# A four-layer graph network on one core: the output stages of the fourth layer spread over two chunks

## The chip, the cores and the metric

The kernel runs on one NeuronCore of a Trainium2 chip. A core has five engines that run their own instruction queues and wait for each other by semaphores: TensorE (PE, matrix products into the accumulator memory PSUM), VectorE (DVE), ScalarE (ACT), GpSimd (POOL), and SyncE (SP), which here only issues transfers. DMA queues move data between the device memory and the on-chip buffers. The metric is the device time of one execution in microseconds (us). The time before is the median of three runs.

## The reference

A graph has N = 12,500 nodes with 32 features and E = 400,000 edges from `src` to `dst`, sorted by `dst`. Four message-passing layers follow each other; each one normalizes the node features, computes something for every edge from its source node, sums it over the edges of each target node, and adds the result to the features. The change concerns the fourth, an equivariant convolution with 8 scalars and 8 three-vectors per node:

```python
h = relu(edge_scalars @ (fc_w1 * (1.0 / sqrt(8)))) * SQRT2      # E x 256
w = (h @ (fc_w2 * (1.0 / sqrt(256)))).reshape(E, 4, 8, 8)       # four 8x8 matrices per edge
x = node_features[edge_src]
s1, v1 = x[:, :8], x[:, 8:].reshape(E, 8, 3)
s2, v2 = edge_sh[:, 0], edge_sh[:, 1:4]
out_s = A_S * (einsum('eu,euw->ew', s1 * s2, w[:, 0]) + C * einsum('eui,ei,euw->ew', v1, v2, w[:, 1]))
out_v = A_V * C * (einsum('eu,euw,ei->ewi', s1, w[:, 2], v2) + einsum('eui,euw->ewi', v1 * s2, w[:, 3]))
node_out = segment_sum(concat([out_s, out_v]), edge_dst) * const
```

So each edge has its own 256 weights, made by a small network from 8 numbers, and uses them on the 32 features of its source node.

## The kernel before

The four layers run one after the other. The fourth is `edges3`. It cuts the edges into NW = 196 chunks of 2048: CT = 16 columns of 128 edges, one edge per partition. A Python loop writes out the work of all chunks; a planner (the framework under the kernel) then sets the order of instructions on each engine. It keeps to the order in which they are written where two are ready by its own estimate of the times, and takes a later one first where the earlier isn't ready. A buffer of a pool is taken again when its last reader is done.

The steps of one chunk `c`:

- `fetch` issues four loads on SP's queue: the source indices `src`, the local target places `local` with the first node of the chunk's window behind them (`places_of`, L466), the four numbers per edge `edge_attr`, and the input of the hidden layer `emb`. They go into a pool of 6 buffers (`load3`).
- `gather` issues 16 indirect DMAs on POOL (L1226), one per column: each partition fetches the 32 features of its edge's source node from device memory into `hs`. There are 4 buffers of `hs`.
- `hidden`, in four steps: two matmuls into `ps_h` (L1237; one buffer of PSUM) and a ReLU by ACT into `hid` (L1239).
- `scalars`: four DVE instructions (L1245 `q`, L1247 `dd`, L1249 `q`, L1251 `vv`) multiply the gathered features with `edge_attr`.
- `product`, in four slots of four columns: eight fp32 matmuls (L1262, sixteen records in the trace) make the 256 weights of 512 edges in `ps_w` (two buffers of PSUM); DVE multiplies them with the features: `pa` (L1266), `ps` (L1268), `pv` (L1270). `pa`, `ps` and `pv` of a chunk fill up over the four slots. `ps` is also the last reader of `hs`: the fourth slot's sets the buffer free for the gather of four chunks later.
- `outputs`: DVE reductions of `pa` (L1278), `pv` (L1279) and `ps` (L1282, into `rs`), a product (L1284, `t1`) and a sum (L1286) make `f`, the 32 numbers per edge.
- `thirds`, four steps: `f` is written as three bf16 parts in `f3`. Step 0: ACT rounds `f` to bf16 (L441). Step 1: DVE takes that away from `f` (L443). Step 2: ACT rounds the rest (L441 again). Step 3: DVE takes that away and writes the third part (L445).
- `places`, in four steps of four columns: ACT makes one-hot rows `oh` of the local target place (L1292 four times, L1293 once).
- `collect`, the range sum: 16 matmuls (L1298) of `f3` and `oh` add the chunk's edges into the 128 nodes of its window, in `ps_sum` (one buffer); ACT copies it (L1301).
- `add`, the fold: a matmul (L1304) adds the three parts, ACT copies the result (L1306), and `put_late` (L456) loads the first node of the window into a register of ACT and writes the window to device memory from ACT's queue (L459).

All pools but those named have two buffers (`rs`, `t1` and `dd` one, `wsum` four).

Iteration `c` of the loop (L1318 on) first calls `fetch` for chunk c + 4 and `gather` for c + 2. Then come four slots, s = 0 to 3. In each, chunk c has its `product` and a quarter of its `places`, chunk c - 1 (`last`) has a part of its output stages, and chunk c + 1 has a step of `hidden` (in slot 3 also `scalars`). The output stages of `last` are written so: slot 0 all of `outputs` and step 0 of the thirds, slot 1 the steps 1 and 2, slot 2 step 3 and `collect`, slot 3 `add`. So a chunk's last write comes one iteration behind its products.

The order in which the trace shows them on DVE, in one chunk period: L1278 and L1279 of `last`, the three products of slot 0, L1282, `pa` of slot 1, L1284, `ps` of slot 1, L1286, `pv` of slot 1, L443, the three of slot 2, L445, L1245 and L1247, `pa` and `ps` and `pv` of slot 3, L1249 and L1251. On PE: the range sum of `last`, the last step of `hidden`, the fold, then product, hidden, product, hidden, product, hidden, product.

Of the kernel before, what the change touches and what calls it, by code (L numbers as in the profile page):

```python
# [8 lines left out]
F32 = mybir.dt.float32  # L9
# [3 lines left out]
ALU = mybir.AluOpType  # L13
AX = mybir.AxisListType
PSUM = bass.MemoryType.PSUM

P = 128
D = 32
# [19 lines left out]
class GNN:  # L38
# [424 lines left out]
            c["first"] = self.nc.values_load(c["wbase"], engines=[mybir.EngineType.SP], min_val=0, max_val=self.N - 1)  # L463
        return c["first"]

    def places_of(self, pool, row):  # L466

        t = pool.tile([P, self.CT + 1], F32, name="local")
        self.nc.sync.dma_start(t, self.local[:, ds(row, 1), :].rearrange("p o t -> p (o t)"))
        return {"local": t[:, : self.CT], "wbase": t[0:1, self.CT :].bitcast(I32)}  # L470

# [732 lines left out]
    def edges3(self):  # L1204

        nc, tc, CT = self.nc, self.tc, self.CT
        with ExitStack() as ctx:
            ld = ctx.enter_context(tc.tile_pool(name="load3", bufs=6))
            gp = ctx.enter_context(tc.tile_pool(name="gather3", bufs=4))
            wp = ctx.enter_context(tc.tile_pool(name="work3", bufs=2))  # L1210
# [4 lines left out]
            def fetch(c):  # L1215
                row = c["no"]
                c["src"] = self.load(ld, "src", c["col"])
                c.update(self.places_of(ld, row))
                c["sh"] = self.load(ld, "edge_attr_4", c["col"])
                c["emb"] = ld.tile([72, Q4 * B], BF16, name="emb")  # L1220
                nc.sync.dma_start(c["emb"], self.emb8[:, :, ds(row, 1), :].rearrange("k f o e -> (k f) (o e)"))

            def gather(c):
                c["hs"] = gp.tile([P, CT, D], F32, name="hs")
                for k in range(CT):
                    nc.gpsimd.indirect_dma_start(  # L1226
                        out=c["hs"][:, k, :], out_offset=None, in_=self.feats[3][:],
                        in_offset=bass.IndirectOffsetOnAxis(ap=c["src"][:, k : k + 1], axis=0))
# [13 lines left out]
            def scalars(c):  # L1242
                hs, sh = c["hs"], c["sh"]
                q = c["q"] = wp.tile([P, CT, 16], F32, name="q")
                nc.vector.tensor_mul(q[:, :, 0:8], hs[:, :, 0:8], sh[:, :, 0:1].to_broadcast([P, CT, 8]))  # L1245
                dd = wp.tile([P, CT, 3, 8], F32, name="dd", bufs=1)
                nc.vector.tensor_mul(dd, hs[:, :, 8:32].rearrange("p g (k u) -> p g k u", k=3),  # L1247
                                     sh[:, :, 1:4, None].to_broadcast([P, CT, 3, 8]))
                nc.vector.tensor_reduce(q[:, :, 8:16], dd.rearrange("p g k u -> p g u k"), AX.X, ALU.add)  # L1249
                vv = c["vv"] = wp.tile([P, CT, 3, 8], F32, name="vv")  # L1250
                nc.vector.tensor_mul(vv.rearrange("p g i u -> p g (i u)"), hs[:, :, 8:32], sh[:, :, 0:1].to_broadcast([P, CT, 24]))  # L1251
# [19 lines left out]
                                     w[:, :, None, 192:256].to_broadcast([P, 4, 3, 64]),  # L1271
                                     c["vv"][:, gs].rearrange("p g i u -> p (g i) u")[:, :, None, :].to_broadcast([P, 12, 8, 8]))

            def outputs(c):
                sh = c["sh"]
                f = c["f"] = wp.tile([P, CT, D], F32, name="f")
                fv = f[:, :, 8:32]
                nc.vector.tensor_reduce(f[:, :, 0:8], c["pa"], AX.X, ALU.add)  # L1278
                nc.vector.tensor_reduce(fv.rearrange("p g (w i) -> p g i w", i=3),  # L1279
                                        c["pv"].rearrange("p g i (w u) -> p (g i) w u", u=8), AX.X, ALU.add)  # L1280
                rs = wp.tile([P, CT, 8], F32, name="rs", bufs=1)
                nc.vector.tensor_reduce(rs, c["ps"], AX.X, ALU.add)  # L1282
                t1 = wp.tile([P, CT, 8, 3], F32, name="t1", bufs=1)
                nc.vector.tensor_mul(t1, rs[:, :, :, None].to_broadcast([P, CT, 8, 3]),  # L1284
                                     sh[:, :, None, 1:4].to_broadcast([P, CT, 8, 3]))
                nc.vector.tensor_add(fv, fv, t1.rearrange("p g w i -> p g (w i)"))  # L1286

            def places(c, k0, k1):
                if k0 == 0:
                    c["oh"] = wp.tile([P, CT, P], BF16, name="oh")  # L1290
                for k in range(k0, k1):
                    nc.scalar.activation(c["oh"][:, k, :], self.iota, AF.Square, bias=c["local"][:, k : k + 1], scale=-1.0)  # L1292
                nc.scalar.activation(c["oh"][:, k0:k1, :], c["oh"][:, k0:k1, :], AF.Relu, bias=self.one, scale=-2.0)  # L1293

            def collect(c):
                c["sum"] = ps.tile([P, B], F32, name="ps_sum")
                for k in range(CT):
                    nc.tensor.matmul(c["sum"][: 3 * D, 0:P], lhsT=c["f3"][:, k].rearrange("p i f -> p (i f)"), rhs=c["oh"][:, k, :],  # L1298
                                     start=k == 0, stop=k == CT - 1)
                c["s4"] = wp.tile([3 * D, P], F32, name="s4")  # L1300
                nc.scalar.copy(c["s4"], c["sum"][: 3 * D, 0:P])  # L1301

            def add(c):
                nc.tensor.matmul(c["sum"][:, P : P + D], lhsT=c["s4"], rhs=self.fold[: 3 * D], start=True, stop=True)  # L1304
                s = wp.tile([P, D], F32, name="wsum", bufs=4)
                nc.scalar.copy(s, c["sum"][:, P : P + D])  # L1306
                self.put_late(3, c, s)

            NW = self.NW
            cs = [{"no": c, "col": c * CT} for c in range(NW)]  # L1310
            for c in range(4):
                fetch(cs[c])
# [2 lines left out]
            for s in range(4):  # L1315
                hidden(cs[0], s % 2, s // 2)
            scalars(cs[0])
            for c in range(NW + 1):  # L1318
                now = cs[c] if c < NW else None
                if c + 4 < NW:  # L1320
                    fetch(cs[c + 4])
                if c + 2 < NW:
                    gather(cs[c + 2])
                for s in range(4):
                    if now:
                        product(now, s)
                        places(now, 4 * s, 4 * s + 4)
                    if c:
                        last = cs[c - 1]
                        if s == 0:  # L1330
                            outputs(last)
                            self.thirds(wp, last, 0)
                        elif s == 1:
                            self.thirds(wp, last, 1)
                            self.thirds(wp, last, 2)
                        elif s == 2:
                            self.thirds(wp, last, 3)
                            collect(last)
                        else:
                            add(last)  # L1340
                    if c + 1 < NW:
                        hidden(cs[c + 1], s % 2, s // 2)
                        if s == 3:
                            scalars(cs[c + 1])
# [151 lines left out]
```

## Time and profile before

| what | value |
|---|---|
| median of 3 runs | 20,968.87 us (20,962.72 to 21,010.88) |
| the profiled execution | 20,866.96 us |
| its span in the profile | 20,865.2 us |
| mean granted clock of TensorE | 0.841 |
| PE, DVE, ACT, POOL busy over the whole span | 61%, 61%, 31%, 71% |
| PE, DVE, ACT, POOL busy in the fourth layer (500 us from 17,500 us) | 74%, 65%, 46%, 57% |
| memory traffic in the fourth layer | 23 GB/s |
| matmuls of the products, L1262, per record | 413 ns mean |
| reductions L1278, L1279, L1282 | 2276, 3340, 1206 ns |
| `pa`, `ps`, `pv` (L1266, L1268, L1270) | 686, 413, 946 ns |
| parts of `f`: L441 (ACT), L443, L445 (DVE) | 606, 690, 680 ns |
| one indirect gather, L1226 | 969 ns |

The shares over the whole span mix four layers with different limits, so they say little on this one. The fourth layer begins some 15,500 us after the start. Durations are those of one instruction from its start to its end; on DVE the next one often starts a little before the end is recorded (0.60 us from the start of `pa` to that of `ps`, 0.33 from `ps` to `pv`), and sums along an engine go by these distances. The ends of matmuls are modelled in the records. "remote" as a releaser stands for a wait whose end the profile can't put down to an instruction of this core.

### The profile page before, as it was taken

How to read it: one execution, taken by the hardware profiler on the slowest of the kernel's cores; microseconds unless marked ns; L12 is line 12 of the kernel's file. 1: busy time of each engine (PE TensorE's matmuls, PEld its weight loads, DVE VectorE, ACT ScalarE, POOL GpSimd, SP SyncE). 2: the span in 40 equal slices, each digit the busy share in tenths (PEclk: the TensorE clock that was granted, in tenths of full speed). 3: DMA queues.
4: the chain of work that ended last, by engine and by line, in shares of the span. 5: the costliest groups of instructions: out<-in, count | busy, mean ns of one | idle time of the engine just before them, and what ended most of it. 6: DMA issues, size and time to landing. Idle time of an engine off the chain costs nothing. (4 is left out here: it accounts for less than half of the span.)

```text
span 20865.2 us, 192054 instructions
## 1 busy us (share of the span) xinstructions
PE 12672.2 (61%) x56452; PEld 6857.3 (33%) x56452; DVE 12731.2 (61%) x25514; ACT 6397.8 (31%) x13844; POOL 14767.1 (71%) x12552
## 2 busy tenths in 40 slices
PE   2433433333766666666666666666637777777776
PEld 2333333331211111111111111111125555655554
DVE  3544444334766666666666666666746666666666
ACT  0001110001333333333333333333314444444443
POOL 5777777774788888888888888888855555555554
PEclk9999999998777777777777777777768888888888
DMA  3123332112444444444444444444421111111111
GB/s 96 43 46 109 114 94 74 24 23 67 97 91 91 91 91 91 90 92 89 92 89 89 91 88 91 89 91 90 87 49 23 24 24 24 24 24 24 24 24 30
DMA packets 1541412, 1407.87 MB, mean 67 GB/s; under 512 B 1114278, under 2 KB 1309952, under 8 KB 1485464
## 3 DMA queue, kind: packets, MB, share of 16 engines
q1 hardware_dynamic: 724998, 1146.69, 17.5%
q0 software_dynamic: 752640, 206.32, 12.7%
q10 hardware_dynamic: 62704, 42.42, 0.7%
q8 instruction: 448, 7.34, 0.1%
q14 instruction: 622, 5.10, 0.1%
HBM read 1157.36 MB, written 236.38 MB: 67 GB/s over the span
## 5 line engine op out<-in xcount | busy, mean ns | idle before, releaser
L965 POOL DMA_INDIRECT acc<-summed,rows x3136 | 5167.0, 1648 | 998.0 <-issue 880.2
L1226 POOL DMA_INDIRECT hs<-feat,src x3136 | 3039.5, 969 | 2356.2 <-DVE ps L1268 1354.8
L494 POOL DMA_INDIRECT hs<-feat,src x3136 | 3359.7, 1071 | 1387.8 <-issue 878.5
L766 POOL DMA_INDIRECT hs<-feat,src x3136 | 3200.1, 1020 | 1196.9 <-issue 940.2
L1262 PE MATMUL ps_w<-w2b,hid 128*128 128x256 f32 x12544 | 3191.5, 411 | 63.4 <-issue 50.2
L810 DVE TENSOR_TENSOR z<-ps_y,hid 128x1024 f32<-128x1024 f32 x2352 | 2834.7, 1212 | 382.5 <-PE ps_y L807 153.0
L807 PE MATMUL ps_y<-X,w2t 64*128 64x512 f32 x4704 | 2384.7, 746 | 1113.9 <-DVE z L810 699.9
L1262 PEld LDWEIGHTS ps_w<-w2b,hid 128*128 128x128 f32 x12544 | 2593.3, 209 | 561.4 <-issue 80.6
L807 PE MATMUL ps_y<-Q,w2t 64*128 64x512 f32 x4704 | 1681.0, 842 | 1644.5 <-DVE z L810 994.3
L429 PE MATMUL ps_win<-m,oh 128*128 128x32 f32 x6272 | 1472.5, 400 | 856.8 <-issue 270.8
L441 ACT CAST f<-f 128x512 bf16<-128x512 f32 x784 | 479.8, 612 | 4770.9 <-DVE f L835 3993.4
L817 PE MATMUL ps_o<-z,sums 128*32 128x512 f32 x9408 | 1758.8, 706 | 23.7 <-DVE r L822 15.8
L429 PEld LDWEIGHTS ps_win<-m,oh 128*128 128x128 f32 x6272 | 1396.3, 328 | 928.7 <-issue 576.6
L648 PE MATMUL ps_deg<-olo,ohi 128*125 128x100 bf16 x3136 | 462.4, 298 | 2007.0 <-DVE olo L645 1232.4
L1266 DVE TENSOR_TENSOR pa<-ps_w,q 128x512 f32<-128x512 f32 x784 | 537.6, 686 | 1624.7 <-remote 1274.2
L781 DVE STREAM_TRANSPOSE X<-hs 128x512 f32<-128x512 f32 x392 | 273.4, 700 | 2035.2 <-DMA hs<-feat,src 1719.1
L1239 ACT ACTIVATE hid<-ps_h 128x1024 f32<-128x1024 f32 x784 | 801.8, 1023 | 2259.3 <-remote 1465.7
L807 PEld LDWEIGHTS ps_y<-Q,w2t 64*128 64x128 f32 x4704 | 523.4, 256 | 2889.5 <-issue 1436.1
L807 PEld LDWEIGHTS ps_y<-X,w2t 64*128 64x128 f32 x4704 | 614.8, 210 | 2326.8 <-DVE z L810 1215.7
L621 DVE TENSOR_TENSOR m<-hs,edge_attr 128x128 f32<-128x128 f32 x784 | 225.9, 288 | 1608.5 <-issue 679.8
L622 ACT ACTIVATE m<-m 128x128 f32<-128x128 f32 x784 | 238.9, 308 | 3084.4 <-DVE m L621 1040.1
L648 PEld LDWEIGHTS <-ohi 128*125 128x125 bf16 x3136 | 446.5, 215 | 1995.9 <-DVE ohi L645 931.6
(206 smaller groups left out, 19755.0 us busy)
## 6 DMA issues: line engine op xcount, KB each, us to landing
has<-loc_t SPq DMA_DIRECT2D x392, 1024.0 KB
srow<-in_src_t SPq DMA_DIRECT2D x392, 512.0 KB
hs<-feat,src POOLq DMA_INDIRECT x9408
N<-n_t SPq DMA_DIRECT2D x3136, 32.0 KB
emb<-pp SPq DMA_DIRECT2D x252, 280.0 KB
emb<-emb SPq DMA_DIRECT2D x196, 360.0 KB
emb<-pp SPq DMA_DIRECT2D x252, 224.0 KB
emb<-emb SPq DMA_DIRECT2D x196, 288.0 KB
```

The source lines that it names most:

```text
L429: nc.tensor.matmul(c["sum"], lhsT=oh[:, k, :], rhs=feat[:, k, :], start=t0 + k == 0, stop=t0 + k == self.CT - 1)
L494: self.nc.gpsimd.indirect_dma_start(out=t[:, k, :], out_offset=None, in_=self.feats[l][:], in_offset=bass.IndirectOffsetOnAxis(ap=idx[:, t ...
L648: nc.tensor.matmul(c["deg"][:NP, :J], lhsT=ohi[:, k, :], rhs=olo[:, k, :], start=t0 + k == 0, stop=t0 + k == self.CT - 1)
L766: nc.gpsimd.indirect_dma_start(out=c["hs"][:, k, :], out_offset=None, in_=self.feats[1][:], in_offset=bass.IndirectOffsetOnAxis(ap=c["src" ...
L807: nc.tensor.matmul(y[:, q, :], lhsT=self.w2t[64 * q : 64 * q + 64, h, j, :], rhs=c["Q" if j < 3 else "X"][64 * q : 64 * q + 64, h, :], sta ...
L810: nc.vector.tensor_mul(z, y, c["hid"][:, 2 * h : 2 * h + 2, :])
L817: nc.tensor.matmul(c["o", j // 3][32 * q : 32 * q + 32, :], lhsT=self.sums[:, j, :], rhs=c["z", j, q % 2][:, q // 2, :], start=j % 3 == 0, ...
L965: nc.gpsimd.indirect_dma_start(out=self.tabs[2][k % NTAB][:], out_offset=bass.IndirectOffsetOnAxis(ap=c["rows"][:, G * g + k : G * g + k + ...
L1226: nc.gpsimd.indirect_dma_start(out=c["hs"][:, k, :], out_offset=None, in_=self.feats[3][:], in_offset=bass.IndirectOffsetOnAxis(ap=c["src" ...
L1239: nc.scalar.activation(c["hid"][:, m, :, 2 * h : 2 * h + 2, :].rearrange("p b q s -> p q b s"), t.rearrange("p q (b s) -> p q b s", s=32), ...
L1262: nc.tensor.matmul(w[:, k, :], lhsT=c["hid"][:, m, 4 * g + k].rearrange("p q s -> p (q s)"), rhs=self.w2b[:, m, :], start=m == 0, stop=m == 1)
L1266: nc.vector.tensor_mul(c["pa"][:, gs], w[:, :, 0:128].rearrange("p g (w u) -> p g w u", u=16), c["q"][:, gs, None, :].to_broadcast([P, 4, ...
```

## The change

The output stages of a chunk are written over two iterations in place of one. In iteration c, `now` is chunk c, `last` is c - 1, `prev` is c - 2:

| slot | before: of `last` | after: of `prev` | after: of `last` |
|---|---|---|---|
| 0 | `outputs` (five instructions), thirds 0 | thirds 3 | places 0 to 3, L1278 |
| 1 | thirds 1, thirds 2 | `collect` | places 4 to 7, L1279 |
| 2 | thirds 3, `collect` | `add` | places 8 to 11, L1282, L1284, L1286, thirds 0 |
| 3 | `add` | | places 12 to 15, thirds 1, thirds 2 |

(In the diff L1278, L1279 and so on keep their instructions; the lines get other numbers.) `places` moves from `now` to `last`, a chunk later. In the text of a slot, `prev` comes behind `product` and ahead of `last`. The loop has one more round. `local` gets eight buffers in place of six, since the first node of a window is now read up to an iteration later; all other buffers keep their numbers.

```diff
--- before.py
+++ after.py
@@ -463,9 +463,9 @@
             c["first"] = self.nc.values_load(c["wbase"], engines=[mybir.EngineType.SP], min_val=0, max_val=self.N - 1)
         return c["first"]
 
-    def places_of(self, pool, row):
-
-        t = pool.tile([P, self.CT + 1], F32, name="local")
+    def places_of(self, pool, row, bufs=None):
+
+        t = pool.tile([P, self.CT + 1], F32, name="local", bufs=bufs)
         self.nc.sync.dma_start(t, self.local[:, ds(row, 1), :].rearrange("p o t -> p (o t)"))
         return {"local": t[:, : self.CT], "wbase": t[0:1, self.CT :].bitcast(I32)}
 
@@ -1215,7 +1215,7 @@
             def fetch(c):
                 row = c["no"]
                 c["src"] = self.load(ld, "src", c["col"])
-                c.update(self.places_of(ld, row))
+                c.update(self.places_of(ld, row, bufs=8))
                 c["sh"] = self.load(ld, "edge_attr_4", c["col"])
                 c["emb"] = ld.tile([72, Q4 * B], BF16, name="emb")
                 nc.sync.dma_start(c["emb"], self.emb8[:, :, ds(row, 1), :].rearrange("k f o e -> (k f) (o e)"))
@@ -1271,13 +1271,17 @@
                                      w[:, :, None, 192:256].to_broadcast([P, 4, 3, 64]),
                                      c["vv"][:, gs].rearrange("p g i u -> p (g i) u")[:, :, None, :].to_broadcast([P, 12, 8, 8]))
 
-            def outputs(c):
-                sh = c["sh"]
-                f = c["f"] = wp.tile([P, CT, D], F32, name="f")
-                fv = f[:, :, 8:32]
-                nc.vector.tensor_reduce(f[:, :, 0:8], c["pa"], AX.X, ALU.add)
-                nc.vector.tensor_reduce(fv.rearrange("p g (w i) -> p g i w", i=3),
-                                        c["pv"].rearrange("p g i (w u) -> p (g i) w u", u=8), AX.X, ALU.add)
+            def outputs(c, step):
+
+                if step == 0:
+                    c["f"] = wp.tile([P, CT, D], F32, name="f")
+                    nc.vector.tensor_reduce(c["f"][:, :, 0:8], c["pa"], AX.X, ALU.add)
+                    return
+                sh, fv = c["sh"], c["f"][:, :, 8:32]
+                if step == 1:
+                    nc.vector.tensor_reduce(fv.rearrange("p g (w i) -> p g i w", i=3),
+                                            c["pv"].rearrange("p g i (w u) -> p (g i) w u", u=8), AX.X, ALU.add)
+                    return
                 rs = wp.tile([P, CT, 8], F32, name="rs", bufs=1)
                 nc.vector.tensor_reduce(rs, c["ps"], AX.X, ALU.add)
                 t1 = wp.tile([P, CT, 8, 3], F32, name="t1", bufs=1)
@@ -1315,8 +1319,8 @@
             for s in range(4):
                 hidden(cs[0], s % 2, s // 2)
             scalars(cs[0])
-            for c in range(NW + 1):
-                now = cs[c] if c < NW else None
+            for c in range(NW + 2):
+                now, last, prev = (cs[c - k] if 0 <= c - k < NW else None for k in range(3))
                 if c + 4 < NW:
                     fetch(cs[c + 4])
                 if c + 2 < NW:
@@ -1324,20 +1328,21 @@
                 for s in range(4):
                     if now:
                         product(now, s)
-                        places(now, 4 * s, 4 * s + 4)
-                    if c:
-                        last = cs[c - 1]
+                    if prev:
                         if s == 0:
-                            outputs(last)
-                            self.thirds(wp, last, 0)
+                            self.thirds(wp, prev, 3)
                         elif s == 1:
-                            self.thirds(wp, last, 1)
+                            collect(prev)
+                        elif s == 2:
+                            add(prev)
+                    if last:
+                        places(last, 4 * s, 4 * s + 4)
+                        if s < 3:
+                            outputs(last, s)
+                        if s > 1:
+                            self.thirds(wp, last, s - 2)
+                        if s == 3:
                             self.thirds(wp, last, 2)
-                        elif s == 2:
-                            self.thirds(wp, last, 3)
-                            collect(last)
-                        else:
-                            add(last)
                     if c + 1 < NW:
                         hidden(cs[c + 1], s % 2, s // 2)
                         if s == 3:
```

## The prediction

> **What bounds the kernel now.** First the page's slices (the span in 40 equal parts of 522 us, each digit a busy share in tenths), to find the fourth layer: the last ten digits, from about 15,500 us to the end of its gathers at 20,707 us.
>
> ```profile
> PE   2433433333766666666666666666637777777776
> ...
> DVE  3544444334766666666666666666746666666666
> POOL 5777777774788888888888888888855555555554
> ```
>
> No engine is full there. Four windows of 500 us inside the layer give one picture; a row holds the busy time of PE, PEld, DVE, ACT and POOL:
>
> ```profile
> 17500.00:18000.00 500.00, 370.52 (x1645) 296.21 (x1644) 323.80 (x421) 232.44 (x509) 285.98 (x295) 0.85 0.13 23
> ```
>
> PE is busy 74%, DVE 65%, POOL 57%, ACT 46%. So a ring of waits sets the pace, and I looked for its period and its members. From one chunk's first gather (L1226) to the next is 27.1 us, to a tenth, in chunk after chunk; 196 chunks of it are 5.3 ms. The waits of 2800 us (17,500 to 20,300, 103 chunks; us in total, times, longest):
>
> ```profile
> ACT hid L1239 <- remote: 776.2, 144, 10.3
> POOL hs L1226 <- DVE ps L1268: 723.3, 103, 7.8
> DVE pa L1266 <- remote: 694.8, 149, 9.5
> ...
> PE ps_sum L1298 <- DVE f L445: 545.6, 99, 8.8
> ```
>
> The change aims at the fourth line: PE stands 545.6/103 = 5.3 us per chunk in front of the range sum, because L445 writes the last bf16 part late. What the reader should see is that the other three are longer, and what they are. The timeline of one chunk shows it (start, duration, engine, line; in brackets the wait and its releaser):
>
> ```profile
> 18979.06 0.94 POOL L1226 DMA_INDIRECT hs<-feat,src  x1 [6.77 <-DVE ps L1268]
> ...
> 18989.81 3.62 PE L1262 MATMUL ps_w<-w2b,hid 128*128 128x256 f32 x16
> ...
> 19001.82 0.69 DVE L1266 TENSOR_TENSOR pa<-ps_w,q 128x512 f32<-128x512 f32 x1 [3.85 <-remote]
> 19001.87 1.02 ACT L1239 ACTIVATE hid<-ps_h 128x1024 f32<-128x1024 f32 x1 [4.61 <-remote]
> ...
> 19003.63 0.68 DVE L445 TENSOR_TENSOR f<-f,f 128x512 bf16<-128x512 f32 x1
> ...
> 19004.36 1.94 PE L1298 MATMUL ps_sum<-oh,f 128*96 128x128 bf16 x16 [4.56 <-DVE f L445]
> ...
> 19004.90 0.68 DVE L1266 TENSOR_TENSOR pa<-ps_w,q 128x512 f32<-128x512 f32 x1
> ...
> 19006.18 0.94 POOL L1226 DMA_INDIRECT hs<-feat,src  x1 [7.09 <-DVE ps L1268]
> ```
>
> The third product's matmuls (18989.81) end by the record at 18993.43; DVE takes the result at 19001.82, 8.4 us later, and the profile finds no releaser ("remote"). ACT's hid is let go in the same moment, though its matmuls are long done. In all chunks that I laid over one another, PE results ready later than about 12 us after a chunk's first gather are seen only 22.7 us after it, a moment behind the last of the sixteen gathers (18998.14, 19.08 us after the first, 0.94 long); results ready before 7.6 us are seen at once. From 19001.82 DVE runs pa, ps, pv, L445, two of the scalars (L1245, L1247), pa, ps, and the fourth ps frees the hs buffer for the next first gather: 19006.18 - 19001.82 = 4.4 us. **The ring is 22.7 us (gathers and the late release) + 4.4 us (DVE) = 27.1 us.** A sign that gathers do it: behind the last one (20,707 us) the reductions of L1278 begin at 20714.94, 20734.31 and 20752.11, so chunks of 19.4 and 17.8 us.
>
> The Trainium skill, "Perfetto Trace Analysis", section "Tensor Engine Instruction (MATMUL, LD_WEIGHTS)", says that the profiler estimates a matmul's end and doesn't observe it. By it PE itself could be the slow part, the 5.3 us would come off the period, and the time would be some 1040 us shorter (an estimate), about 19,930. The rows speak against it: the third product's records end at 18993.43 and those of ACT's hid at 18996.34, and both are let go within 0.05 us.
>
> **The change part by part.** Per chunk no instruction, transfer or matmul is added or dropped; all are moved.
>
> (a) PE's wait for L445 goes, 5.3 us per chunk of PE time. PE is not on the ring at that point: it waits while DVE does its 4.4 us. What goes on next is the fourth hidden matmul and the first product of the next chunk, some 3 us earlier; they then wait for PSUM (two ps_w buffers, freed by the third and fourth pv). Gain on the ring as such: 0; what it could give is in the first rival.
>
> (b) L445 goes from the third slot to the first slot of the next iteration. It lies on the 4.4 us with 0.60 us (19003.63 to the next start, 19004.23). Gain 0.60.
>
> (c) DVE's order. Today the planner puts L1278 and L1279 (2.28 + 3.34 us) ahead of the first pa, L1282 behind the first pv, L1284 and L1286 in between the second trio; all five are written in slot 0. The diff writes L1279 one slot and L1282, L1284, L1286 two slots later. Fully as written, L1282 (1.13 to the next start), L1284 and L1286 (0.47 each) stand between the third pv and the fourth pa: +2.07, with (b) +1.5, ring 28.6. If the planner hoists them all as it hoists today's, none of them does: +0, with (b) -0.6, and without L1245 and L1247 (0.20 + 0.47) there too, -1.3, ring 25.8. Between these: it hoists what is ready when its own clock has DVE idle, and it hoisted today by about one slot; so L1282 and L1284 come ahead of the third product and L1286 stays. +0.47.
>
> (d) L443, 0.60 us, follows the first cast (L441), which follows L1286. With L1286 behind the third product, L443 lands before or behind the fourth pa. Before: +0.60. Today it waits 112.0/104 = 1.1 us per chunk for ACT; on the path that wait would count, 0 to 1.1. I take 0.60 and, as an estimate, 0.13 of the wait.
>
> (e) The cast stands in ACT's third slot, 0.61 us (L441), ahead of a hidden's relu (1.02). ACT is busy 46% and itself waits for the release; cost 0 while that covers it. Queued behind a cast that waits for its f are the relu and with it the next ps_h (one buffer) and product. The same section of the Trainium skill calls ACT and DVE strict FIFO, which speaks against the change; in the trace ACT's order is that of its queue, and the sum by the rule is rival 4.
>
> (f) Sum (1.94 us by its records) and fold (0.47) move to the second and third slot, with copies (0.26, 0.18), the register load and the write on ACT's queue (0.34 us issue). Their data are then an iteration old, so nobody waits for them; they push the third product back by up to 2.4 us, which (a)'s earlier start covers. The places (16 + 4 ACT instructions) are a chunk later and lose nothing. The loads on SP keep their order; only "local" has eight buffers.
>
> (g) One more round at the end: its L445, sum, fold and write were serial there already. 0 to 5 us, taken as 0.
>
> Sum: -0.60 + 0.47 + 0.60 + 0.13 = +0.60 us a chunk, x 196 = +118 us. Against the profiled execution, 20866.96 us (span 20865.2, 1.8 around it), that is 20,985. The median of the runs shown is 20,968.87, 0.49% above the profiled one; so 21,087 there, rounded to 21,085. The likeliest case runs from +0.3 (no measurable change ends there) to (c) as written, +1.5 us per chunk: 21,030 to 21,260.
>
> **The rivals.**
>
> 1. *The third product slips through (faster).* PE starts earlier by (a); the third product is ready at 14.4 us in the chunk shown, about 12 would be wanted. Then DVE does the third trio before 22.7 and only the fourth pa and ps (0.60 + 0.41, and 0.27 until POOL starts) follow: 22.7 + 1.3 = 24.0, or -3.1 x 196 = -600 us at most, 20,370; if it does so in four chunks of ten, -240, 20,730. For: ready 2.4 us too late, start 3 us earlier. Against: the sum and fold now lie in front of it, and its PSUM waits for the first pv, which stands behind the 5.6 us of L1278 and L1279.
>
> 2. *All hoisted (faster).* (c)'s lower bound: -1.3 x 196 = -255 us, 20,715. For: today's order. Against: the text now places them lower.
>
> 3. *The same ring.* What enters the 4.4 us equals what leaves it (L443 for L445): within 0.3 us a chunk, within 60 us of 20,969. 0.3% of 20,969 is 63 us, about what a measurement of this kernel can tell from no change.
>
> 4. *Much slower: the first product is caught.* If the planner keeps L1278 and L1279 behind the first two trios and the cast in front of the relu, the hidden and product chain starts later; a first or second product that is ready after 12 instead of before 7.6 is held to 22.7, and the fourth one then runs after the release with a PE at half clock (matmuls 0.43 us apart instead of 0.22, seen after the waits): 16 x 0.21 = 3.4 more for its sixteen records, with the likeliest case's 0.60 +4.0 x 196 = +785 us, 21,755. It decides when the second product is ready beyond 12 us; today 10.5 (18989.54 - 18979.06), seen 3.0 late.
>
> 5. *It doesn't do what it says.* If L445 of prev still runs right before the sum, the wait stays and the ring too: the time of rival 3, counted there.
>
> **How the numbers follow.** Likeliest 0.42, rival 1 0.15, rival 2 0.13, rivals 3 and 5 0.14, rival 4 0.16. Faster by over 0.3%: 0.28; within: 0.14; slower: 0.58. The range leaves out the deepest half of rival 1 and the outer half of rival 4 (if its hold comes in three chunks of four, +590): 20,500 to 21,560.
>
> **What would show it.** Right: the wait of PE for L445 falls from 545.6 to nearly 0 while POOL's for ps stays, first gathers 27.4 to 28.5 us apart, pa and hid still "remote", the third product seen at 22.7, and L443 or L1286 in front of the fourth pa in the timeline. (a) is wrong if the period falls towards 24 with the third pa ahead of the last gather, (c) if all reductions lie before the third pa, (e) and (f) if PE's products start later than now. The prediction is wrong altogether if gathers are not what holds PE's results, for then the freed 5.3 us count.

## The result, and the profile after

| | before | after |
|---|---|---|
| median of 4 runs | 20,979.38 us (20,962.72 to 21,010.88) | 21,485.1 us (21,466.02 to 21,491.9) |
| ratio | | 1.0241, 95% interval 1.0229 to 1.0253 |
| span of the profiled execution | 20,865.2 us | 21,478.9 us |
| from first gather to first gather, fourth layer, mean of 181 chunks | 27.11 us | 30.29 us |
| chunks rounded to 27 or 28 us | 180 | 58 |
| rounded to 29 or 30 us | 1 | 20 |
| rounded to 31 us or more | 0 | 103 |

The change costs 506 us (2.4%), where 116 were forecast. 3.18 us more per chunk x 196 = 623 us, about the 613.7 by which the spans differ. So all of it lies in the fourth layer, and it is not spread evenly: 58 chunks take about 27.8 us, 103 take 31 us or more.

The waits of the same 2800 us as before (17,500 to 20,300; engine, what waits, what ended it; us in total, times, longest), in the changed kernel:

```profile
ACT s L1305 <- remote: 1251.1, 90, 17.8
POOL hs L1226 <- DVE ps L1268: 963.5, 92, 13.1
DVE pa L1266 <- remote: 810.0, 80, 10.4
...
PE ps_sum L1308 <- ACT s L1305: 479.1, 63, 10.9
```

PE's wait for L445 (545.6 us before) is gone, as the change means it to be. In its place ACT waits 1251 us, 13.9 us each time, with the copy of the range sum (L1305), and PE waits with the fold (L1308) behind it. The gathers wait longer for the fourth `ps` than before (963.5 against 723.3 us, for 92 chunks in place of 103).

The timeline of one long chunk (its first gather starts at 19394.84; start, duration, engine, line, in brackets wait and releaser):

```profile
19394.84 0.95 POOL L1226 DMA_INDIRECT hs<-feat,src  x1 [12.69 <-DVE ps L1268]
...
19402.07 1.06 PE L1302 MATMUL ps_sum<-oh,f 128*96 128x128 bf16 x16
...
19402.97 0.60 PE L1237 MATMUL ps_h<-emb,w1s 72*128 72x512 bf16 x2
...
19403.40 3.65 PE L1262 MATMUL ps_w<-w2b,hid 128*128 128x256 f32 x16
...
19416.85 0.26 ACT L1305 COPY s<-ps_sum 96x128 f32<-96x128 f32 x1 [17.01 <-remote]
...
19417.17 0.64 PE L1308 MATMUL ps_sum<-fold,s 96*128 96x32 f32 x2 [10.11 <-ACT s L1305]
...
19417.58 1.02 ACT L1239 ACTIVATE hid<-ps_h 128x1024 f32<-128x1024 f32 x1 [0.16 <-remote]
19417.74 0.69 DVE L1266 TENSOR_TENSOR pa<-ps_w,q 128x512 f32<-128x512 f32 x1 [10.35 <-remote]
...
19419.46 5.39 PE L1262 MATMUL ps_w<-w2b,hid 128*128 128x256 f32 x16
...
19424.89 0.69 DVE L1266 TENSOR_TENSOR pa<-ps_w,q 128x512 f32<-128x512 f32 x1
...
19426.18 0.94 POOL L1226 DMA_INDIRECT hs<-feat,src  x1 [11.64 <-DVE ps L1268]
```

Three results leave TensorE while the gathers run: the range sum (matmuls done at 19403.13), the second step of the hidden layer (19403.57) and the third product (19407.05). All are seen 22.0 to 22.9 us after the first gather, in this order. Only then can the fold, the third hidden step and the fourth product follow: the third step needs the one buffer `ps_h`, which the second relu sets free, and the fourth product is queued behind it on TensorE. It takes 5.39 us, the first 3.6 of them at a granted clock of 0.5, and the fourth `pa` starts at 19424.89. In the kernel before, the second hidden step's result came out at 10 to 16 us, so the third step and the fourth product ran while results were held, and VectorE found both products ready at the release.

One relation carries the rest. For each chunk from 16,500 us on I took the start of the second hidden step's relu ("second relu"), counted from the chunk's first gather, and the chunk's length:

| second relu starts | chunks before | chunks after | mean length after |
|---|---|---|---|
| by 17 us | 143 of 150 (27.1 us) | 8 of 154 | 27.8 us |
| 17 to 20.5 us | 7 (27.3 us) | 48 | 28.0 us |
| 20.5 to 22 us | 0 | 10 | 30.1 us |
| later | 0 | 88 | 31.8 us (30.9 to 32.8) |

One thing has to be known for the numbers that follow: beside the runs e1 to e8 and e16 the kernel before took 20,850 to 21,017 us, as here, and beside the others 19,003 to 19,050 us, once on the same chip (21,017 and later 19,027), and in the profiles taken with these shorter times hardly a result is held back (at most 2 of the 1,400 to 2,000 of a profile are seen more than 1 us late, against 41 to 49% in the other profiles with all sixteen gathers).

### The profile page after: what moved, and what is told of

The parts are those of the page before. It is cut to its first block, busy times and chain, and to the rows that moved or that the text cites. A ratio compares the mean times of both kernels' runs of the same rounds, so it can differ in the third digit from the quotient of the medians.

```text
span 21478.9 us, 191920 instructions
## 1 busy us (share of the span) xinstructions
PE 12638.1 (59%) x56452; PEld 6782.1 (32%) x56452; DVE 12730.7 (59%) x25514; ACT 6352.5 (30%) x13844; POOL 14711.1 (68%) x12552
## 3 DMA queue, kind: packets, MB, share of 16 engines
q0 software_dynamic: 752640, 206.32, 12.4%
## 5 line engine op out<-in xcount | busy, mean ns | idle before, releaser
L1262 PE MATMUL ps_w<-w2b,hid 128*128 128x256 f32 x12544 | 3273.6, 417 | 266.8 <-ACT hid L1239 158.1
L1262 PEld LDWEIGHTS ps_w<-w2b,hid 128*128 128x128 f32 x12544 | 2658.2, 213 | 897.3 <-ACT hid L1239 211.4
L1296 ACT ACTIVATE oh<-iota,local 128x128 bf16<-128x128 f32 x3136 | 1037.7, 393 | 26.4 <-DMA local<-local 26.3
```

The lines of the kernel that those rows point to most:

```text
L1262: nc.tensor.matmul(w[:, k, :], lhsT=c["hid"][:, m, 4 * g + k].rearrange("p q s -> p (q s)"), rhs=self.w2b[:, m, :], start=m == 0, stop=m == 1)
```

## The experiments

Theory A: the range sum's result is now ready in the middle of the gathers and is one more among those held back, in front of the second hidden step's; where that step's relu comes too late the chunk is long. Theory B: VectorE's longer list between the release and the fourth `ps` is all there is. Runs of one group ran on the same chip, beside the kernel before. Each number is set against the kernel before of its own group.

**e1: the sum in slot 0, the fold in slot 1**

```diff
                         if s == 0:
                             self.thirds(wp, prev, 3)
-                        elif s == 1:
                             collect(prev)
-                        elif s == 2:
+                        elif s == 1:
                             add(prev)
```

> The changed kernel with the range sum of prev in slot 0 (right behind L445) and the fold in slot 1, one slot earlier each. Theory A (a held result in front of two queues): in the changed kernel the sum's matmuls end 8.5 to 9 us after a chunk's first gather, its copy on ACT is let go only at 16 to 22.4 us, and three of the four relus and the third hidden step and last product stand behind it. With the sum ready some us earlier its copy is not held; the chunks of 31 to 32.7 us go and all are like the short ones of now, 27.8 us at most: about 21,000 us (30.3 - 27.8 = 2.5 us x 196 = 490 less than 21,485). Theory B (VectorE's list between the release and the fourth ps has grown by L1290, L1251 and L443 with its wait): the place of the sum doesn't matter, period 30.3 us, about 21,485.

21,354 us (before 21,017; one run of each), mean period 29.54 us: 114 chunks rounded to 28 us, 59 of 31 or more. The copy of the sum is no longer held (4.4 to 5.0 us after the first gather in the short chunks), and most of the chunks are short. But a third of them is still long: now the fold's result is among the held ones (its copy L1310 starts at 16.2 us in the mean). The long chunks also begin slowly: TensorE's granted clock in their first 6 us is 0.58 in the mean, in the short ones 1.00, and the second hidden step is done at 11.5 us in place of 9.0. A half success for A; it was put too simply.

**e2: only the fold later, in slot 3**

```diff
-                        elif s == 2:
+                        elif s == 3:
                             add(prev)
```

> The changed kernel with only the fold moved from slot 2 to slot 3; the sum and its copy on ACT stay. It tells which of the two queues behind the held copy sets the time. Theory A1 (TensorE's queue: the fold waits for the copy, and the third hidden step and the last product stand behind the fold): the products no longer wait for the fold, period 27.5 to 28.5 us, 20,940 to 21,140. Theory A2 (ACT's queue: the relus stand behind the copy): the relus are as late as now, period 29.5 to 30.5 us, 21,330 to 21,525. Theory B: no change, 30.3 us.

21,326 us (before 21,017), period 29.35 us: 309 us over the kernel before, where the change costs 506. The copy is still held (it starts at 17.7 us in the mean); the fold no longer stands in front of the hidden steps, yet TensorE now waits 698.9 us for the relu in 2800 us from 18,000 on. Between A1 and A2, so neither queue alone.

**e3: the copy of the sum on VectorE**

```diff
-                nc.scalar.copy(c["s4"], c["sum"][: 3 * D, 0:P])
+                nc.vector.tensor_copy(c["s4"], c["sum"][: 3 * D, 0:P])
```

> The changed kernel with the copy of the range sum on VectorE in place of ACT. Theory A2 (ACT's queue): the second and third relu are let go as their own results come, before the release, and the period falls to 27.5 to 28.5 us (20,940 to 21,140), though VectorE now waits with the copy. Theory A1 (TensorE's queue): the fold waits as long as now and holds the last product, period 29.5 to 31 us. Theory B: 0.3 us more on VectorE, period 30.3 to 30.6 us.

21,515 us (before 21,017), period 30.40 us. No gain, but the run isn't clean: the planner moved much else (on VectorE L1282 now stands behind the copy, for one), and ACT now waited 912.9 us at the one-hot rows (L1296), whose buffer a held range sum still reads, it seems. It speaks against ACT's copy as the only cause, no more.

**e4: the outputs back in slot 0**

```diff
-                        if s < 3:
-                            outputs(last, s)
+                        if s == 0:
+                            for k in range(3):
+                                outputs(last, k)
```

> The changed kernel with one part undone: all five instructions of the outputs are written in slot 0 again; thirds, range sum, fold and places stay as changed. Theory A: the sum is still ready at 8 us or later and its copy held, period 29.5 to 30.5 us, 21,330 to 21,525. Theory B: the list between the release and the fourth ps is short again, period 27.0 to 27.5 us, 20,850 to 20,960.

21,480 us (before 21,017), period 30.17 us, and the copy is held as long (19.1 us in the mean). As a test of theory B the run is weak: the reductions lie ahead of the third product again, but in their place the planner put L443 and all four scalars behind it, so VectorE's list between the release and the fourth `ps` is no shorter. What speaks against B as the main cause is another thing: VectorE runs the same order in all 181 chunks of the changed kernel, those of 27.8 us and those of 31 us and more, and the same again in e2, which loses less. In e1 to e4 the length follows the second relu as in the table: chunks where it starts by 20.5 us take 27.7 to 28.3 us in the mean, those where it starts after 22 us 31.6 to 33.0.

**e5: the sum behind the fourth product**

```diff
                         if s == 0:
                             self.thirds(wp, prev, 3)
-                        elif s == 1:
-                            collect(prev)
-                        elif s == 2:
-                            add(prev)
+                        elif s == 3:
+                            collect(prev)
+                            add(prev)
...
-                    nc.tensor.matmul(c["sum"][: 3 * D, 0:P], lhsT=c["f3"][:, k].rearrange("p i f -> p (i f)"), rhs=c["oh"][:, k, :],
-                                     start=k == 0, stop=k == CT - 1)
+                    m = nc.tensor.matmul(c["sum"][: 3 * D, 0:P], lhsT=c["f3"][:, k].rearrange("p i f -> p (i f)"), rhs=c["oh"][:, k, :],
+                                         start=k == 0, stop=k == CT - 1)
+                    if k == 0:
+                        tc.keep_in_program_order(m)
```

> The changed kernel with range sum and fold of prev both written in slot 3, and the sum's first matmul kept behind the fourth product on TensorE, so that its result is not among those held back in the middle of the gathers. Theory A (in the changed kernel the sum's result stands in the queue of held results in front of the second hidden step's, and where that step's relu starts after 22 us the chunk takes 31 to 33 us): the second relu starts by 16 us as in the kernel before, the long chunks go, period 27.3 to 28.2 us, 21,020 to 21,190. Theory B (VectorE's longer list between the release and the fourth ps alone): unchanged 30.3 us, about 21,485.

20,844 us (before 20,850; one run of each), period 27.02 us. The whole loss is gone with the place of the sum and its fold (the fold alone was moved in e2, and 309 us of loss stayed). The second relu starts by 17 us in 179 of 181 chunks. The period is even below what was expected, because it is not one value any more: 100 chunks rounded to 28 us, and 40 of about 25 us, in which the third product is seen at 15 to 20 us, ahead of the release. The copy no longer waits on "remote" (98.4 us on other releasers are left); the three longest waits of the 2800 us:

```profile
ACT hid L1239 <- remote: 907.7, 113, 10.5
DVE pa L1266 <- remote: 754.6, 102, 9.7
POOL hs L1226 <- DVE ps L1268: 701.7, 104, 8.3
```

**e6 and e7: no gathers, in both kernels; e8: half of them**

```diff
-                for k in range(CT):
-                    nc.gpsimd.indirect_dma_start(
...
+                nc.sync.dma_start(c["hs"], self.feats[3][0 : P * CT, :].rearrange("(p t) f -> p t f", t=CT))
```

> The kernel before with the sixteen gathers of a chunk in the fourth layer replaced by one plain transfer of 2048 consecutive rows from SP's queue; leaves out the gathering, all else stays. Theory G (gathers hold back what TensorE reports): no wait that ends on 'remote', results seen within 0.1 us, period 18 to 20 us as in the last chunks of the profile before, 19,200 to 19,600. Rival (TensorE itself is late, or its half clock): waits stay, period over 24 us.

> The changed kernel with the same plain transfer in place of the gathers; leaves out the gathering. Theory G: without held results the change does what it is written for, TensorE's wait for L445 is gone and nothing is paid for it: period equal to or up to 2 us below that of the kernel before with the plain transfer. Theory B (VectorE's order is worse as such): 0.5 us or more above it.

> The kernel before with eight of the sixteen gathers of a chunk, the other eight columns by one plain transfer of consecutive rows; leaves out half of the gathering. Theory G: the release comes about 2.6 us after the eighth gather, 10 us earlier than now, at 12.7 us after the first gather; then VectorE and TensorE set the pace, period 18 to 20.5 us, 19,200 to 19,700. Rival (the release is bound to the work of TensorE and not to the gathers): release stays at 20 us or later.

18,973 us for the kernel before and 18,992 us for the changed one (before with its gathers: 20,850). No wait ends on "remote". 140 chunks in the 2500 us from 16,000 on make 17.9 us each in both kernels. Half a millisecond of one of them each (busy time of PE, PEld, DVE, ACT, POOL; then TensorE's clock), first the kernel before with the plain load, then the changed one:

```profile
17500.00:18000.00 500.00, 484.81 (x2529) 385.37 (x2528) 494.95 (x648) 358.32 (x786) 0.00 (x0) 1.00 0.12 35
```

```profile
17500.00:18000.00 500.00, 473.25 (x2526) 392.07 (x2525) 495.63 (x648) 350.19 (x788) 0.00 (x0) 1.00 0.13 35
```

VectorE is busy 99% in both, TensorE's clock is full. So without gathers the layer is bound by VectorE, the change neither removes work from it nor adds any, and its time stays. With eight gathers (e8, 19,204 us) a chunk takes 18.8 us. There the end of a result's matmuls can be set against the semaphore update that it makes: those that end 7 to 9 us after the first gather are late by 1.6 to 2.1 us in the median, those after 12 us not at all. The eighth gather starts at 8.9 us. The hold ends with the gathers and not at a fixed 22.7 us; it ended about 2 us earlier than the 12.7 us expected.

**e9, e10, e13, e14, e16: one extra result in the kernel before**

```diff
+            def extra(c):
+                c["x"] = px.tile([P, D], F32, name="ps_x")
+                return nc.tensor.matmul(c["x"], lhsT=self.w1s[:, 0:P], rhs=c["emb"][:, 0:D], start=True, stop=True)
+
+            def taken(c):
+                return nc.scalar.copy(wp.tile([P, D], F32, name="xc"), c["x"])
...
+                        with tc.issue_after(w.ins):
+                            x = extra(now)
+                        with tc.issue_after(x.ins):
+                            r = hidden(cs[c + 1], 1, 0)
+                        with tc.issue_after(r.ins):
+                            taken(now)
```

(In e9 and e14 `taken` comes ahead of `hidden`, which is queued behind both.)

> The kernel before with one small result more: behind the second product TensorE makes a 128x32 result (one matmul of a step of the hidden layer, cut to 32 columns), and ACT copies it in front of the second hidden step's relu; the copy is read by nothing. Work added: under 0.1 us of TensorE, 0.2 us of ACT. Theory A (one more held result in front of the second relu): the second relu, today at 11 to 16 us after the first gather, slips towards 16 to 23 us; where it starts after 22 us the chunk takes 31 to 33 us; period 28 to 31 us, 21,150 to 21,740 against a before of 20,970. Theory B (only VectorE's list counts): period 27.1 to 27.3 us, within 40 us of the kernel before.

> The same extra result at the same place on TensorE, but ACT copies it behind the second relu. It tells the two ways apart in which the extra result can delay that relu. Theory A2 (the copy waits at the head of ACT's queue): the relu is not behind it, period 27.1 to 27.4 us. Theory A3 (the results leave TensorE one by one and in order, so the hidden step's result comes a place later whoever reads the extra one): the second relu slips as in the other run, period 28 to 31 us.

> The kernel before with one small extra result of TensorE behind the second product, copied by ACT behind the second relu, on a chip with held results (if this is one): A2 (queue of ACT) 27.1 to 27.4 us a chunk, A3 (results leave TensorE in order, one by one) 28 to 31 us. On a chip without held results it tells nothing.

> The same extra result copied by ACT in front of the second relu: A2 and A3 28 to 31 us a chunk on a chip with held results, theory B 27.1 to 27.3 us. On a chip without them it tells nothing.

> The kernel before with one small extra result of TensorE behind the second product, copied by ACT behind the second relu. If the kernel before beside it takes 20,800 us or more (results are held): A2 27.1 to 27.4 us a chunk, A3 28 to 31 us. If it takes about 19,030: a little over 22 us a chunk as the two times before, and nothing on A2 and A3.

e9 (19,343 us) and e10 (19,323, both beside 19,050), e13 (19,289) and e14 (19,279, both beside 19,027) came where nothing is held; they cost 1.3 to 1.5% there, with the copy in front or behind, and say nothing on the question, except that the extra result and its place in the order cost something without any hold. e16 came where results are held: 21,119 us beside 20,980, period 28.28 us against the 27.11 of the kernel before in its profile (one run of each). Every second chunk keeps its 27.2 us, the others take 27.2 to 31.6 us, 29.4 in the median. In one of the long ones:

```profile
18010.45 0.18 PE L1218 MATMUL ps_x<-emb,w1s 72*128 72x32 bf16 x1
...
18010.48 0.59 PE L1245 MATMUL ps_h<-emb,w1s 72*128 72x512 bf16 x2
...
18019.81 1.02 ACT L1247 ACTIVATE hid<-ps_h 128x1024 f32<-128x1024 f32 x1 [8.80 <-issue]
...
18020.73 0.18 ACT L1221 COPY xc<-ps_x 128x32 f32<-128x32 f32 x1
```

The extra matmul takes 0.18 us, and the copy stands behind the relu and can't hold it. Still the relu (its matmuls done at 18011.07) starts 8.7 us later, 19.2 us after the chunk's first gather (18000.58); 10 to 16 us was usual without the extra result. Of 151 chunks 37 have the second relu later than 20.5 us, and those take 29.7 us (20.5 to 22) and 31.2 us (later), as in the changed kernel.

The period alone would not show A3, since the same kernel also loses 1.4% where nothing is held. But second hidden steps that are done at the same time can be compared. Of those whose matmuls end 9 to 11 us after the first gather, the relu starts this much later, in the median:

| in front of the second hidden step stands | chunks | relu later by |
|---|---|---|
| neither (kernel before) | 160 | 3.8 us |
| the extra result (e16) | 90 | 9.9 us |
| the range sum (changed kernel) | 116 | 12.4 us |
| neither, with sum and fold behind the fourth product (e5) | 152 | 0.04 us |

That is A3: one more result in TensorE's line of held results moves those behind it back, whoever reads it. The table shows too that no fixed time after the first gather decides which results are held. A copy in front of the relu (A2) was not tried where results are held.

**e12 and e15: the changed kernel and e5 once more**

> The changed kernel once more, since the runs before showed that the kernel before takes 19,050 us on one chip and 20,850 to 21,020 on the others. Theory A (the loss needs held results): where the kernel before takes about 20,900, the change costs 400 to 600 us as recorded; on a chip where it takes about 19,050 the loss is gone, within 100 us either way. Theory B (VectorE's order): 300 us or more slower on every chip.

> The changed kernel with sum and fold kept behind the fourth product, now with an interval. Theory A, on a chip with held results: within 60 us of the kernel before (one look gave 6 us less), 400 to 600 us below the changed kernel. On a chip without: within 150 us of both.

Both came where nothing is held. The changed kernel: ratio 0.9999, interval 0.9989 to 1.0008 (19,027 against 19,027 us): **no difference at all**. Its 2500 us from 16,000 on:

```profile
POOL hs L1226 <- issue: 582.9, 1913, 0.3
ACT hid L1239 <- DMA local<-local: 570.5, 69, 10.8
DVE pa L1266 <- PE ps_w L1262: 312.2, 99, 8.6
```

The gathers wait for hardly anything but their own issue (8.3 us on other engines and transfers); a chunk takes 20.64 us, little more than 16 x 1.25 = 20.0 us of gathering. Here the stream of gathers is the bound, and the change stays hidden behind it. e15 is 1.0154 (1.0137 to 1.017): keeping the sum behind the fourth product costs here. Its copy then stands waiting at the head of ACT's queue, 650.3 us of the 2100 us from 16,500 on.

**e17 and e18: e5 with an interval, and an order by hand (e11 and e18)**

The order by hand, on TensorE, VectorE and ACT, in the words of its text for chunk c:

```diff
+                relu(c + 1, 2); hmm(c + 1, 3); relu(c + 1, 3)
+                mul(c, 0); mm(c, 1); copy(c - 2); fold(c - 2); places(c - 1, 0, 4)
+                hmm(c + 2, 0); relu(c + 2, 0); mul(c, 1); write(c - 2); places(c - 1, 4, 8)
+                mm(c, 2); hmm(c + 2, 1); relu(c + 2, 1); outputs(c - 1)
+                places(c - 1, 8, 12); thirds(c - 1, 0); places(c - 1, 12, 16); scalars(c + 1)
+                thirds(c - 1, 1); thirds(c - 1, 2); mm(c, 3); mul(c, 2); hmm(c + 2, 2)
+                mm(c + 1, 0); thirds(c - 1, 3); collect(c - 1); mul(c, 3)
```

(`mm` and `mul` are the two halves of `product`, `hmm` and `relu` those of `hidden`, `copy`, `fold` and `write` what follows the sum.)

> A kernel that uses what was found: the fourth layer of the kernel before with the order on TensorE, VectorE and ACT written by hand. The hidden layer runs a chunk further ahead (three buffers of hid), the first product of a chunk is made before the release, the reductions, the scalars and L443 run while results are held back, the sum is last on TensorE before the release, its copy and fold come after it. Same instructions otherwise. Theory A: between the release and the fourth ps VectorE has at most the third and fourth trio and L445: 22.7 + 3.7 = 26.4 us, 20,830; if the third product is seen before the release, 22.7 + 1.3 = 24.0 us, 20,360. Rival (the hold moves with the work, and one result of the hidden chain is caught as in the changed kernel): 27 us or more, 20,950 or more.

> The changed kernel with sum and fold kept behind the fourth product, with an interval. Where results are held (kernel before at 20,800 us or more), theory A: within 0.4% of the kernel before, 2% or more below the changed kernel. Where they are not (19,030): 1.5% slower than before, as measured.

> The order by hand. Where results are held: at most the third and fourth trio and L445 stand between the release and the fourth ps, 26.4 us a chunk (-0.7 x 196 = 140 us less than the kernel before); 24.0 us (-600) if the third product is seen before the release; 27 us or more if a hidden step is caught. Where they are not: 24.0 us, 3.4% slower than before, as measured.

All three came where nothing is held: e11 1.034 (1.0323 to 1.0358), e18 1.0345 (1.0328 to 1.0363), a chunk 23.96 us in e11, and e17 1.0154 (1.0137 to 1.0171). So no version was found that beats both kernels, the order by hand was not timed where results are held, and that the place of sum and fold carries the loss rests there on one run (e5).

## Why the prediction went as it did

The direction was right and the size was not: +116 us forecast, +506 measured, inside the range and outside the likeliest case's own (21,030 to 21,260).

- **The ring of the kernel before** (gathers and late release 22.7 us, then VectorE's list) held. e6 shows that it needs the gathers: without them 17.9 us. They are not enough for it: in e12 the same gathers stream, and nothing is held. That a matmul's recorded end is only an estimate, as the Trainium skill says ("Perfetto Trace Analysis", section "Tensor Engine Instruction (MATMUL, LD_WEIGHTS)"), was not the reason: the trace also has the semaphore updates that TensorE's results make, and set against the records' ends they are more than 1 us late in some 47% of 1699 cases in the kernel before (rough, as some updates are missing there), and in 2 of 1695 in e12, where the changed kernel ran without the hold. Nor was TensorE itself standing still: in the chunk of the prediction the third product's records end at 18993.43, the next hidden step starts at 18995.75 and the fourth product at 18996.18, and the third product is seen at 19001.82.
- **(a)** right: the wait for L445 is gone and gives nothing by itself. Even with plain loads it gives nothing (e7 against e6), since VectorE is full there.
- **(b), (c), (d)** right within a tenth of a microsecond, and measured cleanly in the short chunks: 27.8 against 27.1 us, +0.7 where the sum said +0.60. L445 left the list (-0.60), L1286 (now L1290) stood in it (+0.47), L443 too (+0.60), and L1282 and L1284 (now L1286 and L1288) were hoisted ahead of the third product. In place of a wait of L443 (0.13), L1251 took L1245's place (0.47 for 0.20, +0.27): -0.60 + 0.47 + 0.60 + 0.27 = +0.74.
- **(e)** right nearly to the end: the cast stands behind the late relu and L443 waits for it, 181.7 us in 60 waits of the 2800 us. But in 72 of the 103 long chunks the fourth product is not ready earlier either, in the other 31 by some 0.3 us.
- **(f)** is the step that failed: "Their data are then an iteration old, so nobody waits for them; they push the third product back by up to 2.4 us, which (a)'s earlier start covers." Its data are old, but its own result is new. The sum now ends 8.3 to 8.8 us after the first gather, in the stretch between 7.6 and 12 us in which the prediction itself knew a result that was late (rival 4: ready at 10.5, seen 3.0 late), and ACT waits 13.9 us each time for it. It was priced as matmul time and not as one more result in the held line, with the second hidden step behind it, and that step was not followed to the fourth product, which the sum took as ready at the release. What it cost: chunks of 27.8 us throughout would be +0.7 x 196 = 137 us; the mean is +3.18, so 2.48 x 196, some 486 us of the 623, come from the longer chunks.
- **The rivals.** Rival 4 had the right kind (a result caught, then a product partly at half clock behind the release, 5.39 us long) and for a caught chunk nearly the right price (+4.0 us forecast, 31.75 - 27.11 = +4.6 in the mean of the 103), but named the first or second product as the one caught and a late start as its cause. It was the second hidden step, caught behind the sum. Rival 1's condition came: the third product is now done 12.2 to 12.7 us after the first gather in nine chunks of ten, where about 12 were wanted. Its effect did not: the third `pa` starts at 22.6 us or later in all 181 chunks. So the prediction's reading of two fixed times (before 7.6 us seen at once, after 12 us held) was too simple. An early third product came in e5, ahead of 21.5 us in 67 of 181 chunks. Rival 3's number, no change, is what happens where nothing is held (e12), though not for its reason.

## What to carry to other kernels

When results of an engine are reported late or in a trickle, count each result that falls into that stretch as a place in a line, however small its work; a reduction moved off the critical path can move a result into it. Follow a chain of steps that go back and forth between two engines to its end, not only the instruction that was moved. And before tuning the order of a stage, look which engine would bound it without the waits: here VectorE, full at 17.9 us per chunk, would have given the change nothing either way.

## What the runs showed of the hardware

- While sixteen indirect gathers stream (20 us) and the hold is on, most of what TensorE finishes from about 8 us after the first one on is seen late (13.7 us for the range sum of the chunk shown) and in order; results come out singly until 3 to 4 us after the last gather's start, when the rest comes within 1 us. How late a result is depends on what stands in front of it: a second hidden step done at 9 to 11 us is seen 0.04 us later in e5, 3.8 in the kernel before and 12.4 in the changed one (medians). With eight gathers the lateness ends at about 11 us after the first, with none there is none. VectorE and ACT see each other's results in the same stretch at once (in the kernel before L443 starts 0.03 us after the end of the cast it waits for, 18 us after the first gather).
- The Trainium skill says that PE and ACT never wait on anyone ("SBUF — State Buffer", section "Who interferes with whom"), and that is about the memory's ports. The rows here show another thing that is disturbed while the gathers stream, TensorE's reports, while its matmuls run through in the records (the held third product of the long chunk in 3.65 us).
- The hold comes and goes: the same kernel before took 21,017 us and later 19,027 us on the same chip, and the changed one, 21,485 us in the first comparison, took 19,027 there. What decides it, and by which path the gathers reach TensorE's reports, was not found. A single comparison made in the one condition would have called this change a loss of 2.4%, in the other nothing.
